# Two graph layers on one core: the order of transposes, reloads and stores at the end, and of gathers before the first regrouped batch

## The chip, the cores and the metric

The kernel runs on one core of a Trainium2 chip. The metric is the device time of one execution in microseconds (us), the median of several runs. A profiled execution is one more run with the hardware profiler on; its span goes from the first to the last instruction. Engines are named as in the profile: PE (TensorE, with PEld for its weight loads), DVE (VectorE), ACT (ScalarE), POOL (GpSimd) and SP (SyncE). A small q behind a name (SPq, ACTq, POOLq) is that engine's queue issuing a DMA.

## What is computed

Per batch (32 of them), x is 512 rows by 512 columns, f32. Two layers, each with a norm and a relu ahead and a residual add behind:

```
h = max(layernorm(x), 0);  x = x + (adj @ h) @ W0 + b0          # layer 0
h = max(layernorm(x), 0)
scores = q @ k.T / 8 + (1 - adj) * -1e9                         # per head
x = x + (softmax(scores) @ v) @ Wo + bo                         # layer 1
```

adj holds values from 0 to 1 off a sparse pattern. In layer 1 the mask weighs every missing piece of adj with 1e9, so each row attends to the one column where its adj is largest (the kernel looks at the data and takes this path only where the gap is wide enough). Layer 1 is then a choice of rows: row i gets `h[idx[i]] @ (Wv @ Wo)` plus a constant row, which the kernel calls `cvo`.

## The kernel before, in words

Rows sit on the 128 partitions, so a batch of x is four tiles of 128x512 ("chunks"). `xs` holds five batches of x in SBUF, `X[b] = xs[b % 5]`.

**Stages of a batch b.** Norm of x, then `aggregate` (adj @ h, into `yT`), then `layer0` (yT @ W0, added onto x), then the second norm into `h1`. `put_h` stores h1 to DRAM (`hs_d`). Only some 336 of the 512 rows are ever chosen by layer 1, so `get_h` reads these alone back into `hc`, `transpose_h` turns them on DVE, and `layer1` computes z for them. `put_z` turns z on DVE and stores it to DRAM (`z_d`) with four DMAs for each of two pieces of columns; `finish` gathers z rows by index onto x, and `store` writes x out.

**Products.** Most products go through `product` (L524 to L558), a fast scheme of seven pieces of eight matmuls: p1, p5, u2, c11, c22, c12, c21, in three PSUM banks u, v, w. c21 accumulates on u, so its matmuls (L528) wait until c22 has been taken out of u by DVE (`take_onto` L584 for layer 0, `take_z` L574 on DVE and L576 on ACT for layer 1).

**The order.** It is written out by hand. For each loop turn b, `put(batch, step, f)` hangs work on one of 21 steps: 0 to 6 lie in `layer0(b)`, 7 to 13 in `aggregate(b + 1)`, 14 to 20 in `layer1(b - 1)`. The work of step i is issued after the matmuls of piece i and ahead of the taking of piece i. Each engine runs its own instructions strictly in that order. Every POOL gather or scatter is also tied by `behind` to the taking of the piece before it.

**Regrouped batches.** Batches 0 to 4 (`FIRST` is 4) use x in its natural order. Later ones gather the rows of x in an order found on the chip (`plan.xi`), in which adj has empty blocks; `spread` (L645, L648, L651) then multiplies only `plan.ap` (four chunks of adj regrouped) and `plan.ag` (three small extra tables), with `HG`, the normed form of three extra gathered chunks `plan.gx`. `tables` and `tables_g` (L1282) gather ap and ag, `load_g` (L495) gathers gx, `mask_g` (L1331) blanks the unused part of ag on DVE. `lead` (norm for batches 5 and 6) and `NormMore` (from 7 on) norm gx on ACT: their sums are L394 and L997, the offset L404/L405, the relu L379/L1010.

**The end.** For the last batches x is put back to natural order: `turn_back` scatters X[b] to DRAM (`xn_d`, L468, on POOL) and `come_back` loads it again (L478, on SP). In turn 31, after `layer0(31)`, the seven pieces of `layer1(29)` and then of `layer1(30)` run. There is no further layer 0, so layer 1 of batch 31 is done row by row: `put_h(31)` stores h (L679), `get_all` gathers the chosen rows of h for all 512 rows (L495, `h<-hs,pi`), `transpose_all(r)` turns a chunk on PE (L711) and copies it out on ACT (L712), and `layer1_rows` multiplies (L723) and adds onto x (L728), after `add_cvo` (L715) has added the constant row. In between it adds the z of batches 29 and 30, which `fetch` gathered into `sel` and `yT` (`add_z`, L784), and every finished chunk is stored by SP (L510).

Of the kernel before, what the change touches and what calls it, by code (L numbers as in the profile page):

```python
# [408 lines left out]
def single_path(ctx: ExitStack, tc: tile.TileContext, x, adj, out, kept, room):  # L409
    nc = tc.nc  # L410
    B, N, D = x.shape
    C, DC = N // P, D // P
# [44 lines left out]
    def run_phase(batches, sparse, small, ps_m, ps_t):  # L457
# [256 lines left out]
        def add_cvo(b, c):  # L714
            nc.vector.tensor_add(X[b][:, c, :], X[b][:, c, :], cvo)  # L715

        def layer1_rows(b):
            for r in range(C):
                bank = ps_m.tile([P, D], F32, name="mm")
                for d in range(DC):  # L720
                    if d == 2 and r + 1 < C:
                        transpose_all(r + 1)
                    nc.tensor.matmul(bank, hs[1][:, d, r * P:(r + 1) * P], wvo[:, d, :], start=(d == 0),  # L723
                                     stop=(d == DC - 1))
                if sparse:
                    add_cvo(b, r)
                x_r = X[b][:, r, :].rearrange("p (q c e) -> p q c e", q=4, c=4)
                nc.vector.tensor_add(x_r, bank.rearrange("p (c q e) -> p q c e", q=4, c=4), x_r)  # L728
                if sparse and r == 0:
                    for c in range(C):  # L730
                        add_z(B - 3, c, nc.sync)
                    fetch(B - 2)
                store_rows(b, r, nc.sync)
                for i in range(2):
                    if not sparse:
                        add_z(B - 3 + r // 2, 2 * (r % 2) + i, nc.sync if r < 2 else nc.scalar)
                    elif 0 < r < C - 1:
                        add_z(B - 2, 2 * r - 2 + i, nc.sync)
# [24 lines left out]
        def put_z(b, s0, s1):  # L763
            zr = hc_t if b == B - 2 else zr_t
            nc.vector.transpose(zr[:, s0:s1, :].rearrange("p s (c e) -> p s c e", c=4),
                                zt(b)[:, :, 32 * s0:32 * s1].rearrange("p c (s j) -> p s c j", j=32))
            rows = z_d[b % 3].rearrange("(s j) (q f) -> q j s f", j=32, q=4)
            for q in range(4):
                eng = nc.scalar if q > 1 and b == B - 2 else nc.sync
                eng.dma_start(rows[q][:, s0:s1, :], zr[32 * q:32 * q + 32, s0:s1, :])  # L770

        def place_of(b, c):
# [31 lines left out]
        for b in batches:  # L804
            todo = [[] for _ in range(21)]

            def put(batch, step, f, *args):
                if 0 <= batch < B:
                    todo[step].append(lambda: f(batch, *args))

            if sparse and b <= FIRST + 1:
                for j in range(3):
                    put(b + 1, 1 + j, lambda b, j: lead.stats(j), j)
                put(b + 1, 3, lambda b: lead.power())
                put(b + 1, 4, lambda b: lead.offset())
                for j in range(3):
                    put(b + 1, 4 + (j + 1) // 2, lambda b, j: lead.relu(j), j)
            if sparse:
                for j, step in enumerate((15, 17, 19) if b == FIRST else (6, 7, 8) if b == FIRST + 1 else (4, 5, 6)):
                    put(b + 2, step, load_g, [j])  # L820
# [10 lines left out]
                put(b + 2, 0, load_x)  # L831
            if b == B - 1:
                for c in range(C):
                    put(b - 2, 17 + c if sparse else 15, fetch, [c])
            elif b < B:
                for c, step in enumerate((9, 11, 13, 15) if sparse and b == FIRST + 1 else (7, 9, 11, 13) if sparse else
                                         (4, 5, 6, 7) if ordered and b == FIRST - 1 else (1, 2, 3, 4)):
                    put(b - 2, step, finish, [c])
            elif not sparse:
                put(b - 2, 1, fetch)  # L840
# [2 lines left out]
            if b > 0 and not sparse and not (ordered and b > FIRST - 3):  # L843
                put(b + 3, 15, load_x)
            if ordered and b == FIRST - 1:
                for j in range(3):
                    put(b + 2, 18 + j, load_g, [j])
            if not sparse:
                for i, step in enumerate((0, 1, 2, 3) if b != 1 else (1, 2, 3, 4)):
                    put(b + 1, step, h0_sum, i)  # L850
# [36 lines left out]
            if b < B - 1:  # L887
                put(b, 20 if not several else 17, get_h)
            elif not sparse:
                put(b, 13, get_all)  # L890
                for c in range(C):
                    put(b, 15 + c, add_cvo, c)
            elif b == B - 1:
                for c in range(C):
                    put(b, 13 + c, get_all, [c])
                    put(b, 7 + c, turn_back, [c])
                    put(b - 1, 2 * c, turn_back, [c])
                put(b - 1, 8, come_back)
                put(b, 15, come_back)
            if sparse and b == B - 2:  # L900
                for c in range(C):
                    put(b - 1, c, turn_back, [c])
# [10 lines left out]
            if b == 0:  # L913
                put(2, 1, lambda b: ahead.append(ln0(b, kind)))
                for c, step in enumerate((1, 1, 2, 2)):
                    put(2, step, lambda b, c: ahead[0].stats(c), c)
            else:
                put(b + 2, 4 if sparse else 8, lambda b: ahead.append(ln0(b, kind)))
                for c, step in enumerate((9, 10, 13, 13)):
                    put(b + 2, step, lambda b, c: ahead[0].stats(c), c)  # L920
                if kind is NormMore:
                    put(b + 2, 4, lambda b: ahead[0].more(plan.gx, plan.HG, 3))
                    for i, step in enumerate((13, 15, 17, 17, 18, 18)):
                        put(b + 2, step, lambda b, i: ahead[0].more_stats(i), i)
                    put(b + 2, 20, lambda b: ahead[0].more_power())
            put(b + 2, (17 if sparse else 15) if b > 0 else 11, lambda b: ahead[0].power())
# [10 lines left out]
                    put(0, 8, lambda b, i: sum_b(nc, w0_t, w0_s, i), i)  # L937
                    put(0, 9, lambda b, i: sum_a(nc, wvo_t, wvo, i), i)
            if b == B - 1:
                put(b, 19, lambda b: transpose_all(0))  # L940
            if b == 1:
                tables = []
                put(1, 0, lambda b: tables.append(places()))
# [73 lines left out]
class Plan:  # L1017
# [315 lines left out]
    def schedule(self):  # L1333
        def at(b, step, f, *args):
            self.steps.setdefault(b, []).append((step, lambda ps_t, behind: f(*args)))

        def pe(b, step, f, *args):
            self.steps.setdefault(b, []).append((step, lambda ps_t, behind: f(ps_t, *args)))

        def move(b, steps, f):  # L1340
            for i, step in enumerate(steps):
                self.steps.setdefault(b, []).append((step, lambda ps_t, behind, i=i: f(behind, i)))

        at(0, 0, self.load)
        at(0, 0, self.constants)
        at(0, 3, self.constants2)
        for c in range(4):
            at(0, 3 + c // 2 * 4, self.nonzero, c)
            at(0, 8 + c // 2, self.nonzero_t, c)
        at(0, 8, self.key_r)  # L1350
        for c in range(4):
            at(0, 11, self.diagonal, self.m, c)
            at(0, 12, self.diagonal, self.mt, c)
        pe(0, 11, self.rank_pe)
        at(0, 12, self.pick_r)
        k = 21
        for r in range(2):
            for go, then in ((self.sources, self.known), (self.reach, self.key_1), (self.rank_pe, self.pick_1),
                             (self.rank_pe, self.pick_2)):
                pe(*divmod(k, 21), go)  # L1360
                at(*divmod(k + 1, 21), then)
                k += 3
        at(*divmod(k - 1, 21), self.classes)
        pe(*divmod(k, 21), self.sources)
        at(*divmod(k + 1, 21), self.outside)
        k += 3
        pe(*divmod(k, 21), self.numbers)
        for i, f in enumerate((self.positions, self.positions_2, self.positions_3, self.slots)):
            at(*divmod(k + 1 + min(i, 2), 21), f)
        pe(*divmod(k + 4, 21), self.row_pe, self.pos)  # L1370
        at(*divmod(k + 5, 21), self.row_save, self.posd)
        for c in range(4):
            at(*divmod(k + 4 + c // 2, 21), self.place_onehot, c)
            at(*divmod(k + 6 + c // 2, 21), self.slot_onehot, c)
        k += 9
        pe(*divmod(k, 21), self.lists)
        at(*divmod(k + 1, 21), self.indices)
        move(2, (17, 18, 19, 20), self.rows)
        for m in range(4):
            pe(3, 4 + m, self.turn, m)  # L1380
        at(3, 6, self.save_at, 0)
        at(3, 8, self.save_at, 2)
        move(3, (11, 13, 15, 17), self.tables)
        move(4, (0, 1, 2), self.tables_g)
        for j in range(3):
            at(4, 4 + j, self.mask_g, j)
        move(5, (14, 16, 18, 20), self.look_1)
        at(6, 4, self.whole_pi)
        pe(6, 5, self.row_pe, self.pqf)
        at(6, 6, self.row_save, self.tab2)  # L1390
        move(6, (14, 16, 18, 20), self.look_2)
        at(7, 5, self.packed, self.pq, self.place)
        at(8, 5, self.packed, self.pi, self.home)
# [261 lines left out]
```

## Time and profile before

| | us |
|---|---|
| median of three runs | 1024.74 (1020.9, 1024.74, 1027.37) |
| the profiled execution's own time | 1019.28 |
| its span | 1017.5 |
| start and end around the span | 1.8 |
| PE busy, and its share of the span | 990.3, 97% |
| DVE busy | 801.1 |
| ACT busy | 585.5 |
| POOL busy | 589.7 |

From turn 6 to turn 30 one loop turn takes 28.82 us. The DMA engines are busy in eight to nine tenths of most slices. PE's granted clock is full except for three stretches (from 235.2 us for 3.4 us, from 986.1 us for 6.8 us, and the last 7 us). The page's rows give, for a group of instructions, the busy time, the mean of one in ns, and the idle time ahead of them with what ended it.

### The profile page before, as it was taken

To read this page: it belongs to the slowest core of one execution; us is meant where nothing else is said; L and a number is where in the kernel's file an instruction comes from. 1 tells how busy PE (TensorE), PEld (TensorE's weight loads), DVE (VectorE), ACT (ScalarE), POOL (GpSimd) and SP (SyncE) were. 2 spreads that over 40 slices of the span, in tenths; PEclk is the share of its full clock that TensorE was granted. 3 is DMA by queue.
4 is the path that set the end of the run, shared out by engine and by line. 5 is a ranking of instruction groups with operands and counts; after the bars stand their busy time and mean duration, and the time that the engine had idled before them with its cause. 6 is when DMAs were issued, how large, how long until landed. Compare 5 with 4: busy or idle time off the path is not lost.

```text
span 1017.5 us, 17277 instructions
## 1 busy us (share of the span) xinstructions
PE 990.3 (97%) x5627; PEld 888.4 (87%) x5627; DVE 801.1 (79%) x1792; ACT 585.5 (58%) x1282; POOL 589.7 (58%) x666
## 2 busy tenths in 40 slices
PE   8999999998999999999999999999999999999986
PEld 7468888898999999999999999999999999999872
DVE  5998888667888777778887777778887777788754
ACT  3766455556765555567655555667655555676230
POOL 1033266656666666666666666666666666666552
PEclk9999999999999999999999999999999999999988
DMA  9314668888887888898888888888888888888886
GB/s 297 114 65 134 119 191 233 211 220 223 223 206 187 215 221 207 226 223 216 213 195 205 214 215 214 227 220 216 202 195 213 215 206 226 227 214 216 204 302 224
DMA packets 163035, 210.99 MB, mean 207 GB/s; under 512 B 16684, under 2 KB 104504, under 8 KB 162936
## 3 DMA queue, kind: packets, MB, share of 16 engines
q0 software_dynamic: 44544, 120.10, 48.5%
q1 hardware_dynamic: 116920, 88.29, 29.9%
q10 hardware_dynamic: 1472, 1.41, 0.4%
q8 instruction: 46, 0.75, 0.3%
q14 instruction: 53, 0.43, 0.2%
HBM read 124.60 MB, written 85.14 MB: 206 GB/s over the span
## 4 chain that ended last, share of the span: by engine, by line
PE 75%; DMA 5%; DVE 2%; ACT 2%; issue 1%; POOL 0%; SPq 0%; POOLq 0%; DVEq 0%
PE mm L528 53%; PE mm L648 13%; PE mm L651 7%; PE mm L645 2%; DMA z<-hc 1%; DMA hc<-hs 1%; DMA at<-in_x_dram,gi 1%; DMA ap<-in_adj_dram,xi 1%; DMA yT<-z,phome 1%; DMA z<-zr 1%; ACT h L379 1%; DMA hs<-h,dest 0%; ACT yT L656 0%; DMA x<-xn 0%; ACT ph L394 0%
## 5 line engine op out<-in xcount | busy, mean ns | idle before, releaser
L584 DVE TENSOR_TENSOR x<-mm,x 128x512 f32<-128x512 f32 x217 | 148.7, 686 | 133.9 <-PE mm L528 131.8
L495 POOL DMA_INDIRECT x<-z,pplace x96 | 153.4, 1598 | 81.8 <-ACT yT L656 40.9
L379 ACT ACTIVATE h<-x,off,rstd 128x512 f32<-128x512 f32 x256 | 196.1, 804 | 7.1 <-DVE off L370 3.9
L528 PE MATMUL mm<-w_t,sel 128*128 128x256 f32 x744 | 171.6, 380 | 1.0 <-DVE x L584 1.0
L365 ACT ACTIVATE rstd<-mv,eps 128x2 f32<-128x2 f32 (+1 forms) x90 | 26.3, 292 | 247.8 <-DVE mv L362 247.7
L361 DVE BATCH_NORM_STATS2 st<-x 128x6 f32<-128x512 f32 x234 | 157.6, 673 | 2.5 <-DMA x<-in_x_dram 1.5
L528 PEld LDWEIGHTS mm<-w_t,sel 128*128 128x128 f32 x744 | 140.7, 190 | 21.0 <-DVE x L584 2.0
L648 PE MATMUL mm<-ap,h 128*128 128x256 f32 x648 | 157.8, 380 | 0.0
L495 POOL DMA_INDIRECT x<-in_x_dram,xi x108 | 103.7, 960 | 73.8 <-DVE x L584 38.4
L512 POOL DMA_INDIRECT out_dram<-x,xi x96 | 120.4, 1254 | 37.3 <-DVE zs L574 20.8
L648 PEld LDWEIGHTS mm<-ap,h 128*128 128x128 f32 x648 | 114.9, 191 | 11.1
L495 POOL DMA_INDIRECT at<-in_x_dram,gi x81 | 76.7, 946 | 74.5 <-DVE st L361 26.3
L528 PE MATMUL mm<-w_s,yT 128*128 128x256 f32 x496 | 117.3, 379 | 0.8 <-ACT zs L576 0.8
L528 PE MATMUL mm<-hTs,wvo_t 128*128 128x168 f32 x720 | 115.0, 309 | 2.9 <-ACT zs L576 2.1
L528 PEld LDWEIGHTS mm<-hTs,wvo_t 128*128 128x128 f32 x720 | 106.5, 192 | 3.9 <-ACT zs L576 3.0
L576 ACT ACTIVATE zs<-mm,cvo_c 128x168 f32<-128x168 f32 x240 | 83.0, 398 | 39.0 <-PE mm L528 38.6
L528 PEld LDWEIGHTS mm<-w_s,yT 128*128 128x128 f32 x496 | 92.8, 190 | 12.3 <-ACT zs L576 1.0
L651 PEld LDWEIGHTS mm<-ag,adjT 128*128 128x128 f32 x648 | 89.3, 191 | 5.6
L651 PE MATMUL mm<-ag,adjT 128*128 128x128 f32 x648 | 89.7, 275 | 0.0
L623 DVE TENSOR_TENSOR x<-x,b_r 128x512 f32<-128x512 f32 x124 | 84.0, 678 | 0.0
L528 PE MATMUL mm<-hT,wvo 128*128 128x168 f32 x480 | 78.6, 307 | 0.0
L656 ACT COPY yT<-mm 128x512 f32<-128x512 f32 x108 | 61.6, 571 | 28.1 <-PE mm L651 27.9
(323 smaller groups left out, 1682.4 us busy)
## 6 DMA issues: line engine op xcount, KB each, us to landing
hc<-hs SPq DMA_DIRECT2D x124, 176.0 KB, 5.7
z<-zr SPq DMA_DIRECT2D x120, 96.0 KB, 3.9
hs<-h SPq DMA_DIRECT2D x52, 192.0 KB
z<-zr SPq DMA_DIRECT2D x120, 80.0 KB, 2.9
hs<-h SPq DMA_DIRECT2D x52, 160.0 KB, 3.0
out_dram<-x SPq DMA_DIRECT2D x32, 256.0 KB, 3.1
x<-in_x_dram SPq DMA_DIRECT2D x12, 256.0 KB, 4.4
x<-xn SPq DMA_DIRECT2D x12, 256.0 KB, 5.0
```

The lines of the kernel that those rows point to most:

```text
L361: self.nc.vector.bn_stats(st, self.src[:, self.chunks[i], :])
L365: self.nc.scalar.activation(self.rstd[:, 0:len(self.chunks)], self.mv[:, :, 1], AF.Sqrt, bias=self.eps)
L379: self.nc.scalar.activation(dst, src, AF.Relu, bias=self.off[:, i:i + 1], scale=self.rstd[:, i:i + 1])
L495: return behind(nc.gpsimd.indirect_dma_start(out=dst, out_offset=None, in_=rows, in_offset=bass.IndirectOffsetOnAxis(ap=at, axis=0), **more))
L512: stored = behind(nc.gpsimd.indirect_dma_start(out=out_rows, out_offset=bass.IndirectOffsetOnAxis(ap=plan.xi[:, b, c:c + 1], axis=0), in_= ...
L528: nc.tensor.matmul(bank[:, m, 0:half], lhs[:, k, m * P:(m + 1) * P], rhs[:, k, :], start=(first and m == 0 and k == 0), stop=(k == 1), ski ...
L576: taken = nc.scalar.activation(dst[:, m, :], bank[:, m, :], AF.Identity, bias=cvo_c[:, 2 * i + m:2 * i + m + 1])
L584: return nc.vector.tensor_add(dst, bank, dst)
L623: nc.vector.tensor_add(X[b][:, c, :], X[b][:, c, :], b0_r)
L648: nc.tensor.matmul(two(bank, j), H0[b][:, j, cols], two(plan.ap[:, j, :], j), start=False, stop=False, skip_group_check=True)
L651: nc.tensor.matmul(bank[:, j * P:(j + 1) * P], extra[:, j - 1, cols], plan.ag[:, j - 1, j * P:(j + 1) * P], start=False, stop=(j == C - 1) ...
L656: tick(nc.scalar.copy(yT[:, d, :], bank))
```

## The change

1. Turn 3 (`b == FIRST - 1`): `load_g(5)` goes from steps 18, 19, 20 to 15, 17, 18; the third and fourth gather of `tables` go from steps 15 and 17 to 19 and 20.
2. Turns 4 and 5: the offset of `lead` goes from step 4 to 5, its relus from 4, 5, 5 to 5, 6, 6 (the relu of j is at the first step plus (j + 1) // 2).
3. Turn 5: the first two of the extra sums of `NormMore` go from steps 13 and 15 to 15 and 16.
4. Turn 31: all four `get_all` at step 13 (13 to 16 before); `come_back(30)` from step 8 to 16; the four `fetch(29)` at step 20 (17 to 20 before); `transpose_all(0)` from step 19 to turn 32; `come_back(31)` from step 15 to turn 32.
5. Turn 32, step 1: `transpose_all(0)`, `come_back(31)` and all four `add_cvo(31)`, which leave `layer1_rows`.
6. `put_z(30)`: all four stores of a piece on SP; two of them were on ACT.

```diff
@@ layer1_rows
-                if sparse:
-                    add_cvo(b, r)
                 x_r = X[b][:, r, :].rearrange("p (q c e) -> p q c e", q=4, c=4)
@@ put_z
-                eng = nc.scalar if q > 1 and b == B - 2 else nc.sync
+                eng = nc.scalar if q > 1 and b == B - 2 and not sparse else nc.sync
@@ run_phase
-                put(b + 1, 4, lambda b: lead.offset())
+                put(b + 1, 5, lambda b: lead.offset())
                 for j in range(3):
-                    put(b + 1, 4 + (j + 1) // 2, lambda b, j: lead.relu(j), j)
+                    put(b + 1, 5 + (j + 1) // 2, lambda b, j: lead.relu(j), j)
...
-                    put(b - 2, 17 + c if sparse else 15, fetch, [c])
+                    put(b - 2, 20 if sparse else 15, fetch, [c])
...
             if ordered and b == FIRST - 1:
-                for j in range(3):
-                    put(b + 2, 18 + j, load_g, [j])
+                for j, step in enumerate((15, 17, 18)):
+                    put(b + 2, step, load_g, [j])
...
-                    put(b, 13 + c, get_all, [c])
+                    put(b, 13, get_all, [c])
                     put(b, 7 + c, turn_back, [c])
                     put(b - 1, 2 * c, turn_back, [c])
-                put(b - 1, 8, come_back)
-                put(b, 15, come_back)
+                put(b - 1, 16, come_back)
...
-                    for i, step in enumerate((13, 15, 17, 17, 18, 18)):
+                    for i, step in enumerate((15, 16, 17, 17, 18, 18) if b == FIRST + 1 else (13, 15, 17, 17, 18, 18)):
...
             if b == B - 1:
-                put(b, 19, lambda b: transpose_all(0))
+                put(b, 20, lambda b: None if sparse else transpose_all(0))
+            if sparse and b == B:
+                put(b - 1, 1, lambda b: transpose_all(0))
+                put(b - 1, 1, come_back)
+                for c in range(C):
+                    put(b - 1, 1, add_cvo, c)
@@ Plan.schedule
-        move(3, (11, 13, 15, 17), self.tables)
+        move(3, (11, 13, 19, 20), self.tables)
```

## The prediction, on record before the result

> **What bounds the kernel now.** I read the page first: PE is busy 97% of the span, so only time in which PE stands still, or work after its last matmul, can be won. The waits of PE say where it stands still; the three largest all lie in stretches that the change touches (waits, count, longest):
>
> ```profile
> PE pt L711 <- DMA h<-hs,pi: 4.8, 1, 4.8
> PE mm L528 <- ACT zs L576: 2.8, 2, 2.1
> PE mm L528 <- DVE x L584: 2.5, 3, 1.5
> ```
>
> The timeline (start, duration, engine, in brackets the idle time ahead and what ended it) shows the 1.5 us in turn 4:
>
> ```profile
> 185.89 0.63 ACT L394 ACTIVATE ph<-at 128x512 bf16<-128x512 f32 x1 [2.69 <-DMA at<-in_x_dram,gi]
> ...
> 189.29 0.18 DVE L404 RECIPROCAL rstd<-rstd 128x3 f32<-128x3 f32 x1 [2.99 <-ACT rstd L401]
> ...
> 189.77 0.68 DVE L584 TENSOR_TENSOR x<-mm,x 128x512 f32<-128x512 f32 x1
> ...
> 190.51 1.99 PE L528 MATMUL mm<-w_t,yT 128*128 128x256 f32 x8 [1.49 <-DVE x L584]
> ```
>
> The gx gathers land late, ACT's sums end late, DVE waits 2.99 us in lead's offset, and the taking of c22 queued behind it holds PE's c21. In turn 5 an extra sum (L997) sits on ACT ahead of p1's taking (L576), for which u2 waits:
>
> ```profile
> 233.71 0.63 ACT L997 ACTIVATE adjT<-at 128x512 f32<-128x512 f32 x1
> ...
> 234.80 0.69 ACT L576 ACTIVATE zs<-mm,cvo_c 128x168 f32<-128x168 f32 x2
> ```
>
> At the end it is no longer PE that counts. PE stands still 4.8 us for the h gather, but what closes the span is a row of transfers and the DVE adds behind them:
>
> ```profile
> 983.71 0.98 POOL L495 DMA_INDIRECT h<-hs,pi  x1 [8.08 <-DMA z<-zr]
> 984.89 0.84 DVE L765 STREAM_TRANSPOSE hc<-h0s 128x640 f32<-128x640 f32 x1 [0.30 <-POOL h0s L760]
> 988.79 1.11 PE L711 MATMUL pt<-ident,h 128*128 128x128 f32 x4 [4.81 <-DMA h<-hs,pi]
> 989.70 2.45 PE L528 MATMUL mm<-adjT_s,wvo 128*128 128x168 f32 x8
> 990.16 0.83 ACTq L770 DMA_DIRECT2D z<-hc  x2
> 992.91 0.98 DVE L765 STREAM_TRANSPOSE hc<-h0s 128x768 f32<-128x768 f32 x1 [7.17 <-ACT h0s L576]
> 998.65 1.18 POOL L495 DMA_INDIRECT yT<-z,phome  x1 [5.15 <-DMA z<-hc]
> 1007.32 0.69 DVE L784 TENSOR_TENSOR x<-yT,x 128x512 f32<-128x512 f32 x1 [2.38 <-DMA yT<-z,phome]
> 1011.32 0.69 DVE L728 TENSOR_TENSOR x<-mm,x 128x512 f32<-128x512 f32 x1
> ```
>
> c21 of layer1(30) sits on PE behind the stalled transposes; z of 30 needs c21; the yT gather needs z; the last adds need yT. Between 264 and 956 us PE has no gap over 0.25 us: time won before stays won there.
>
> **Part 1, the gx gathers sooner, offset a step later (turns 3 and 4).** POOL issues the same seven gathers, spaced as before; gx gets the slots of 172.6, 175.7 and 177.0 us, the last two tables those of 178.2 and 179.5. A gather issued at 176.96 landed at 181.6, so ACT's six sums run from 178.4 to about 184 and the 2.99-us wait goes. Next late is mask_g(0), also ahead of c22's taking: its ag gather ends at 188.42 by the trace's completion events, and its slot is not moved. So 188.5, plus 0.19 to the taking's start, 0.68, 0.06: c21 starts near 189.4 instead of 190.51, **-1.1**. Offset and relus then stand ahead of c12's taking, which no early matmul needs; mask_g(2), for which L651 waits, comes at about 192.7, and PE gets to L651 at 192.8. Cost of the late tables: they land like the gathers now in their slots, by 187.3; L645 needs ap from 191.2, so 3.9 us of cover. Were it gone, PE would wait the difference. DVE has 0.3 us of offset put into its chain, so the stores of h(4) come only 0.8 sooner, and by 223 us (`hc<-hs` landing) that chain leads: **-0.8** carried on. Bounds: 0 (ag later) to -1.4.
>
> **Part 2, turn 5.** Without L997 ahead of it, p1's taking starts 0.6 sooner (ACT still has the yT copy at 234.33): u2 at 235.54 - 0.8 - 0.6. **-0.6**; the sum then delays p5's taking, needed only by c12. The shifted offset of turn 5 saves under 0.3 where DVE waits 1.62 for L401; taken as 0. Here a rule bears on it. The clock row:
>
> ```profile
> 235.20:238.60 3.40, 3.06 (x11) 3.06 (x12) 3.34 (x6) 1.98 (x7) 2.93 (x4) 0.50 1.00 184
> ```
>
> (PE, PEld, DVE, ACT, POOL busy, granted clock, DMA share, GB/s): half clock, so u2 and c11 took 3.87 us for 2.28 at full clock, 1.6 lost. The Trainium skill ("TensorE: Matmul & The Clock Gate", Part 1) has the half rate come after an idle window of some 3.4 us; by that a gap of 2.06, or of 1.5, shouldn't trip it, and nothing is to be won. The trace differs: 2.06 and 0.70 within one such time were enough. With 1.5 and 0.7 left it may go either way; I take a fifth, **-0.3**, bounds 0 to -1.6. Early stages together -1.7.
>
> **Part 3, the end.** (a) `come_back(30)` out of the way of h: four loads of 262 KB, 1.05 MB, ran ahead of `hs<-h` in SP's queue at 396 GB/s (976 to 981 us): 2.6 us. Scatters of xn share the engines, so I take 2.3: gather of h at 981.4 (bounds 1.0, 2.6). (b) c21 follows c12 at once: 983.9 for 989.70, taken by ACT by 986.0. (c) The blanking of h0s (L760) was behind one h gather on POOL and now is behind four, 1.27 each: 986.4, and z's first transpose waits for it, 1.5 later than now. Both transposes (0.84 and 0.98) end at 988.3 instead of 993.9. (d) Eight z stores on SP. The skill ("DMA: Bandwidth & Descriptors", Queues, rings and completion order) says each DMA engine takes turns between the queues it has work for, which speaks against this part: ACT's two stores had a queue of their own, now they stand behind come_back(30)'s 1.05 MB, issued from 981.5. By the rule that costs up to 2.7 us against a free queue; by the rows ACT's pair came out only at 990.16, behind the copy after the stalled transposes, and the second at 993.92. I take issues from 987.4 to 991, landing at 994.3 (now 997.9; the last issue at 995.10 took 2.8, I allow 3.3). (e) fetch(29) starts on POOL at 986.6 (now 988.79), so POOL is free; fetch(30) at 995, **3.7 sooner**. (f) `come_back(31)` goes from 983.44 behind the z stores to 991.5: x(31) lands near 997. DVE now has four add_cvo (0.68 each) queued ahead of all adds of `layer1_rows`, and they wait for it: row 0 at 997.3 (now 996.51). From there DVE does row 0, four adds of z(29) (2.5), row 1, two adds of z(30), row 2, two, row 3: 4 x 0.69 + 2.5 + 2.5 = 7.8, if yT is there: 1005.1; yT's last piece at about 1005.3 (now by 1009.3, less 3.7) makes it 1006.6. PE starts rows at 988 and needs 16 (991.7 to 1007.7 now): 1004, covered. Last store issued at 1006.7 for 1012.04, **-5.3**. (g) Twelve stores of 262 KB need 0.67 each at 390 GB/s, 8.1; from 999.3 with 0.5 MB of yT still to come (1.3), and some idle: 1009.3 for 1014.5. I take **-4.7** for the end: bounds -1 (x(31) at 1001) and -7 (transfers without a gap: 11.6 MB from 974 on at 390 GB/s are 29.7 us, plus some 3.5 for z's short pieces, 1007.5).
>
> **Sum.** -1.7 - 4.7 = -6.4 on the span, 1017.5 to 1011.1; the profiled execution has 1.8 around it, 1019.28 to 1012.9. The median of the runs shown is 5.5 above the profiled one, so 1024.74 - 6.4 = **1018.3**.
>
> **Rivals.**
> *Transfers bound the tail.* The same bytes are moved, nothing fewer. For: the DMA share is 1.04 from 976 to 981 and 1.00 from 986 to 991. Against: 0.63 from 996 to 1001, 0.65 after 1006, room to fill. If queues collide so that yT is only 1.5 sooner, the end gives 2 and the early part 1.7: 1021.
> *More than counted.* The clock stays full in turn 5 (1.3 more) and the tail closes at its bound (2.3 more): 1014.7 or lower. Against: DVE's chain alone needs until 1005.
> *Slower: x(31) too late.* Every add of the last layer now waits behind add_cvo, and x(31) behind eight z stores and a reload. On the present axis the end is then x(31)'s landing plus 0.7 + 7.8 + 2.5 and about 3 to the span's end: it is 1017.5 when x(31) lands at 1003.5, and with the early 1.7 it decides against the change from 1005.2, 8.2 later than I count. If z's eight stores slip behind the reload and the fetches until 1005 and x(31) with them to 1008, the span grows by 2.8 and the time is near 1027.5. Against: in the present run loads issued at 983.44 landed within six us among the same gathers.
> *It doesn't do what it says in the early part.* ag instead of gx holds DVE and `hc<-hs` leads anyway: early 0, end 4.7, 1020; inside the main range.
>
> **How the numbers follow.** Main case (early and end as summed, with its own range 1015.5 to 1021) 56%; transfer-bound tail 19%; more than counted 17%; x(31) late 8%. The spread between runs, 0.6% (1020.9 to 1027.37) lies on top. The range 1012.5 to 1025.5 leaves out the worst of the late case and the best of "more than counted". About 1% is what a measurement of this kernel tells from no change: faster needs under 1014.5, most of the "more" case and a little of the main, 18%; slower needs over 1035, only far in the late case, 5%; the rest 77%.
>
> **What would show it.** Right: c21 of layer0(4) near 189.4; u2 of turn 5 near 234.1; c21 of layer1(30) at about 983 with no transposes ahead; the first yT gather near 993 to 995 on the new axis; first out store near 996 to 999 and the last near 1005. Wrong: a wait of DVE's L715 on `x<-xn` past 1000, a PE wait on ap at L645, or an hs gather not sooner than 983.

## The result, and the profile after

| | before | after |
|---|---|---|
| median of 22 runs each, one chip | 1023.1 | 1022.93 |
| range | 1018.38 to 1027.37 | 1018.11 to 1028.14 |
| ratio, 95% interval | | 1.0003 (0.9986 to 1.0019) |
| profiled execution, its span | 1019.28, 1017.5 | 1018.11, 1016.4 |

No change: not the 6.4 us less that were forecast. Two later measurements of the same two kernels (below) gave 0.997 and 0.9978, some 2 to 3 us less. The bulk of the forecast is missing in all three.

The waits of PE after. The 4.8 us for the h gather are gone, and 1.5 us of waiting for the copy of the transposes are left; but the two rows on the takings are as long as before:

```profile
PE mm L528 <- ACT zs L576: 3.1, 3, 1.7
PE mm L528 <- DVE x L584: 2.8, 3, 1.7
...
PE mm L723 <- ACT h L712: 1.5, 1, 1.5
```

The end, from three answers of the timeline of after (POOL, PE, DVE), with what answers to the rows shown of before:

```profile
980.63 1.02 POOL L495 DMA_INDIRECT h<-hs,pi  x1 [5.71 <-DVE zr L763]
...
997.66 0.95 POOL L495 DMA_INDIRECT yT<-z,phome  x1 [5.16 <-DMA x<-xn]
```

```profile
984.45 1.30 PE L528 MATMUL mm<-adjT_s,wvo 128*128 128x168 f32 x8
985.59 0.60 PE L711 MATMUL pt<-ident,h 128*128 128x128 f32 x4
987.72 1.98 PE L723 MATMUL mm<-wvo,h 128*128 128x512 f32 x4 [1.54 <-ACT h L712]
```

```profile
987.09 1.70 DVE L763 STREAM_TRANSPOSE hc<-h0s 128x640 f32<-128x640 f32 x2
998.25 2.64 DVE L715 TENSOR_TENSOR x<-x,cvo 128x512 f32<-128x512 f32 x4 [9.46 <-DMA x<-xn]
1000.82 0.68 DVE L726 TENSOR_TENSOR x<-mm,x 128x512 f32<-128x512 f32 x1
...
1007.48 0.68 DVE L726 TENSOR_TENSOR x<-mm,x 128x512 f32<-128x512 f32 x1
```

The h gather starts 3.1 us sooner, c21 5.2 sooner (984.45 for 989.70), but the first yT gather only 1.0 sooner. (Its bracket names `x<-xn`, but what it waits for is z: in every profile it starts 0.8 to 1.0 us after the last store of z(30) has landed, whenever x(31) lands.) DVE, which did rows and adds from 996.5 on, stands 9.5 us for x(31) and starts its last chain at 998.25; row 0 comes 4.3 us *later*. The last store is issued at 1009.93 for 1012.04.

The early turns of this execution hold something that no other profile here has: takings that start late though PE is done. DVE at 216.91 takes c11, whose matmuls (214.03, 1.89 long) had ended a microsecond before; it had idled 3.64 us, and PE then waits 1.74 for the PSUM bank:

```profile
214.03 1.89 PE L528 MATMUL mm<-w_s,yT 128*128 128x256 f32 x8
216.91 1.29 DVE L584 TENSOR_TENSOR x<-mm,x 128x512 f32<-128x512 f32 x2 [3.64 <-PE mm L528]
217.66 1.99 PE L528 MATMUL mm<-w_t,sel 128*128 128x256 f32 x8 [1.74 <-DVE x L584]
```

Such takings stand at 150, 173 to 177, 217, 255, 594 and 973 to 986 us. Turns 3 and 6 (from the first matmul of `layer0` to that of the next) were 37.9 and 30.9 us long for 36.1 and 28.9 in a later profile of the same kernel. The trace of this one is also incomplete: it lacks a seventh of PE's completion events (1099; the others have 1291 to 1295), a quarter of ACT's and two fifths of those of the DMAs (9866, where the others have 16338 to 16429), so what its brackets name is less sure than elsewhere. And this execution, at 1018.11 us, is the fastest of its 22, so the late takings are not what makes that median high. They recur in none of the fourteen profiles that follow, so I don't put them down to the change. Whether they are the chip's, the profiler's or chance stays open.

### The profile page after: what moved, and what is told of

It reads as the page before. It is cut to its first block, busy times and chain, and to the rows that moved or that the text cites. A ratio compares the mean times of both kernels' runs of the same rounds, so it can differ in the third digit from the quotient of the medians.

```text
span 1016.4 us, 17276 instructions
## 1 busy us (share of the span) xinstructions
PE 987.2 (97%) x5627; PEld 886.0 (87%) x5627; DVE 800.8 (79%) x1792; ACT 585.5 (58%) x1282; POOL 590.3 (58%) x666
## 3 DMA queue, kind: packets, MB, share of 16 engines
q10 hardware_dynamic: 704, 1.05, 0.3%
## 4 chain that ended last, share of the span: by engine, by line
PE 86%; DVE 5%; DMA 3%; ACT 2%; issue 1%; SPq 1%; DVEq 0%; ACTq 0%
PE mm L528 60%; PE mm L648 13%; PE mm L651 7%; PE mm L645 2%; PE mm L271 1%; PE mm L669 1%; PE mm L150 1%; DMA x<-in_L_gnn_Wv_dram 1%; DMA ap<-in_adj_dram,xi 1%; ACT h L379 1%; DVE st L361 1%; DMA x<-xn 1%; DMA x<-z,place 1%; DMA hc<-hs 0%; DVE x L623 0%
## 5 line engine op out<-in xcount | busy, mean ns | idle before, releaser
L495 POOL DMA_INDIRECT at<-in_x_dram,gi x81 | 77.5, 957 | 69.2 <-DVE st L361 22.8
L576 ACT ACTIVATE zs<-mm,cvo_c 128x168 f32<-128x168 f32 x240 | 83.1, 399 | 41.0 <-PE mm L528 30.4
L656 ACT COPY yT<-mm 128x512 f32<-128x512 f32 x108 | 61.6, 571 | 30.4 <-PE mm L651 30.2
```

What stands on the lines that cost most here:

```text
L495: return behind(nc.gpsimd.indirect_dma_start(out=dst, out_offset=None, in_=rows, in_offset=bass.IndirectOffsetOnAxis(ap=at, axis=0), **more))
L576: taken = nc.scalar.activation(dst[:, m, :], bank[:, m, :], AF.Identity, bias=cvo_c[:, 2 * i + m:2 * i + m + 1])
L656: tick(nc.scalar.copy(yT[:, d, :], bank))
```

## The experiments

Ratios are to the kernel before, run beside it (its medians there: 1018.6 to 1019.6 us). Times "at the end" count from the issue of the second store of h (`hs<-h`, L679; 976.24 before, 975.52 after), so that the early turns drop out; landings are read from the trace's completion events (16 to a DMA).

### The two halves: e1_early, e2_end

e1_early is the kernel before with parts 1 to 3; e2_end has parts 4 to 6 only.

> The kernel before with parts 1 to 3 alone (turns 3 to 5); the end as before. Theory A (the early sum holds, and the end gives it no loss): 1.7 us less than before, ratio 0.998, with c21 of layer0(4) starting some 1.1 us sooner relative to turn 3, and layer0(5) to layer0(7) some 1.7 sooner than before. Theory B (the early stages give back what they win: the profile after shows layer0(4) 1.8 and layer0(5) 2.5 us quicker, but turn 3 slower by 2.0 and turn 6 by 2.0, where takings start 0.5 to 2.5 us after PE is done): if these late takings come from the change they stand at the same places here (173 to 180 us, 217 us, 255 us) and the time is that of before within 0.5 us; if they are chance of one execution, they are gone or stand elsewhere, and the first turns show theory A's numbers.

> The kernel before with parts 4 to 6 alone (the end); the early turns as before. Theory A (x(31) comes late and DVE is parked at add_cvo, so the end wins 0.3 us instead of 4.7): within 0.7 us of before; the last store is issued at most 2.5 us sooner, DVE stands some 9 us ahead of add_cvo. Theory C (the end wins its 4 to 5 us and the early part loses them): 4 to 5 us less than before, ratio 0.9955, and DVE's wait ahead of add_cvo is short.

Measured: e1_early 0.9982 (0.997 to 0.9993), that is -1.8 us; e2_end 0.9992 (0.9974 to 1.001), -0.8. Theory A in both. The early steps by their rows in e1_early: the mask, not the offset, stands last ahead of c22's taking, and c21 follows with no gap:

```profile
188.33 0.29 DVE L1331 TENSOR_SCALAR ag<-ag,valid 128x128 f32<-128x128 f32 x1 [1.63 <-DMA ag<-atd,gi]
188.53 0.68 DVE L584 TENSOR_TENSOR x<-mm,x 128x512 f32<-128x512 f32 x1
189.13 0.17 DVE L404 RECIPROCAL rstd<-rstd 128x3 f32<-128x3 f32 x1
189.27 1.99 PE L528 MATMUL mm<-w_t,yT 128*128 128x256 f32 x8
```

In turn 5 the taking of p1 is ahead of the sum; the wait for hT's sums is 1.20 here for 0.70 before:

```profile
231.34 1.38 PE L528 MATMUL mm<-hTs,wvo_t 128*128 128x168 f32 x8 [1.20 <-DVE hTs L341]
...
233.43 0.69 ACT L576 ACTIVATE zs<-mm,cvo_c 128x168 f32<-128x168 f32 x2
234.01 0.64 ACT L997 ACTIVATE adjT<-at 128x512 f32<-128x512 f32 x1
234.18 1.41 PE L528 MATMUL mm<-hTs,wvo_t 128*128 128x168 f32 x8 [1.45 <-ACT zs L576]
```

Over the profiles (first matmul of `layer0` to the next), turn 4 takes 30.68 and 31.02 us in the two without the early parts and 29.45 in the mean of thirteen with them (28.9 to 30.9: the late gathers vary); turn 5 takes 33.76 and 33.68, and 32.77 (31.7 to 35.4). The wait for hT's sums is no constant either: 0.36 to 1.96 us in the thirteen, 0.58 and 0.70 in the two.

### Where the end is held: e3_rows, e4_back

e3_rows puts add_cvo back, e4_back loads x(31) ahead of z(30)'s stores:

```diff
# e3_rows
+                if sparse:
+                    add_cvo(b, r)
                 x_r = X[b][:, r, :].rearrange(...)
...
-                for c in range(C):
-                    put(b - 1, 1, add_cvo, c)
# e4_back
                 put(b - 1, 16, come_back)
+                put(b, 17, come_back)
...
-                put(b - 1, 1, come_back)
```

> The changed kernel with add_cvo put back into the loop of rows (one ahead of each row's add), come_back(31) still behind the eight stores of z(30). Theory A1 (what costs is that DVE does four add_cvo in a row before anything else): first store some 2 us sooner, the time 1 to 2 us less than the changed kernel. Theory A2 (what costs is that x(31) itself is loaded late; each add_cvo waits for the load either way): DVE still stands some 9 us ahead of the first add_cvo, the first store comes 1.5 to 2 us sooner (three add_cvo fewer ahead of it) but the end moves by less than 1 us, since the stores after it are bound by transfers. Theory C (transfers bound the tail): no change.

> The changed kernel with come_back(31) right behind come_back(30), ahead of the stores of z(30). Theory A2 (late x(31) is what ate the end's gain): x(31) lands near 989 us, DVE no longer waits ahead of add_cvo, row 0 is added by about 993 for 1000.8, out stores start some 7 us sooner and fill the gap in the transfers, and the span ends 3 to 5 us sooner than that of the changed kernel: ratio to before 0.995 to 0.997. Theory C (transfers bound the tail, the same bytes in another order): within 1 us of the changed kernel. Against A2: z(30)'s stores would then wait for 1.05 MB more ahead of them (up to 2.7 us), and fetch(30) with them, which would leave a gain of 1 us or none.

Measured: 0.9967 (0.9954 to 0.9979) and 0.9973 (0.9957 to 0.999). In e3_rows DVE still waits 8.1 us for x(31); the first store comes 2.3 us sooner at the end than in a0_after (22.3 for 24.6), the last one when it did (34.1 for 33.9): A2's numbers. But e4_back, which cures the late x(31) (row 0 at 20.3 for 23.3 in a0_after, the unaltered change), doesn't win A2's 3 to 5 us: its end is 39.8 against 40.3. There z(30) pays. The waits of SP's queue in e4_back:

```profile
SPq L768 <- DMA x<-xn: 6.1, 7, 1.3
```

Seven of z(30)'s eight stores wait, each for the landing of a load: the program hands SP's and ACT's DMAs eight semaphores in turn (100 to 107 in the trace), so a ninth is issued only when the eighth before it has landed. The last store goes out at 19.7 for 14.6, and the first yT gather at 23.0. So late x(31) and late z(30) are two chains of about the same length, and curing one of them brings little.

### The whole change again: a0_after, a1_after

> The changed kernel once more, on the chip of these runs, with a new profile. Parts 1 to 3 alone gave 0.9982 and parts 4 to 6 alone 0.9992. If the parts add up (theory A), the whole is at 0.997 to 0.998 of before here, and its profile has no takings that start 0.5 to 2.5 us after PE is done. If the first comparison (1.0003, interval 0.9986 to 1.0019) holds as it stands, the parts get in each other's way: 1.000, and the late takings at 173 to 180, 217, 255 and 973 to 986 us are there again (theory B).

> The changed kernel a third time. Its first comparison gave 1.0003 (0.9986 to 1.0019), its second 0.997 (0.9957 to 0.9982), and the sum of its two halves 0.9974. If the second holds: 0.996 to 0.998, and a profile without takings that start late. If the first holds: 0.999 to 1.001, and the late takings are there again.

Measured: 0.997 (0.9957 to 0.9982) and 0.9978 (0.9964 to 0.9992); the halves added give 0.9974. No taking starts late in either profile. The 1.0003 of the first measurement lies outside both intervals, though its own (from 0.9986 on) overlaps that of a1_after; there the kernel before, too, took 4 us more, and I have no run that says why.

### What delays z(30): e5_z_act, e6_back30_late, e7_no_back30, e9_no_fetch29, e11_fetch29_last

All five start from e3_rows. e7_no_back30 leaves out the reload of x(30) and e9_no_fetch29 the gathers of fetch(29); both do less than the kernel must, and only measure a time.

```diff
# e5_z_act
-                eng = nc.scalar if q > 1 and b == B - 2 and not sparse else nc.sync
+                eng = nc.scalar if q > 1 and b == B - 2 else nc.sync
# e6_back30_late (e7_no_back30: the first line alone)
-                put(b - 1, 16, come_back)
+                put(b - 2, 1, come_back)      # turn 32, behind come_back(31)
# e9_no_fetch29 (and e11_fetch29_last)
-                    put(b - 2, 20 if sparse else 15, fetch, [c])
# e11_fetch29_last, layer1_rows: behind fetch(B - 2), and after the last row
-                    for c in range(C):
-                        add_z(B - 3, c, nc.sync)
+                    fetch(B - 3)
...
+                    elif r == C - 1:
+                        add_z(B - 3, 2 * i, nc.sync)
+                        add_z(B - 3, 2 * i + 1, nc.sync)
```

> The kernel with add_cvo in the loop of rows, and the third and fourth store of each piece of z(30) on ACT's queue again (part 6 undone). Theory Q (in SP's queue the eight stores stand behind the reload of x(30) and wait for free places, and so land late): on ACT's queue four of them are out sooner, z(30) lands 1 to 2.5 us sooner, the first yT gather starts that much sooner, and the span ends 0.5 to 2 us sooner than with all on SP. Theory C (the DMA engines are busy all the time from the h gathers to the last store, so that an order of transfers moves little): the first yT gather moves by less than 1 us and the span by less than 0.5 us.

> The kernel with add_cvo in the loop of rows, and come_back(30), 1.05 MB, put behind the stores of z(30) and behind come_back(31). Theory Q: the stores of z(30) have nothing ahead of them in SP's queue, land some 2.5 us sooner, and fetch(30) with them; the span ends 1 to 2.5 us sooner. Theory C: the 1.05 MB are only moved to where they stand in the way of the yT gathers and of the first out stores; the first yT gather comes sooner, the last one lands when it did, and the span moves by less than 0.7 us either way.

> The kernel with add_cvo in the loop of rows, and come_back(30) left out: x(30) keeps its regrouped order, so that the output of batch 30 isn't the reference's; 1.05 MB less are moved in the tail. Theory C (transfers bound the tail): the span ends by about the time of these loads sooner, 2.0 to 2.7 us. Theory A2 (the chain of x(31), adds and stores bounds it): less than 0.7 us. The same as with come_back(30) put late, if its place is what matters (theory Q).

> The kernel with add_cvo in the loop of rows, and the four gathers of fetch(29) left out: sel isn't filled, so that the output of batch 29 isn't the reference's, and 1.05 MB less are moved, from POOL's queue, at the time at which z(30) is stored. It measures the disputed term: how long z(30)'s stores take to land. With come_back(30) left out they still took 6.5 us from the last issue to the first yT gather. If the gathers of fetch(29) are what stretches them: 3.3 to 4 us, as in the kernel before, and the first yT gather 2 us sooner. If the short pieces of the stores themselves set it, or x(31): 5.5 to 6 us as now.

> The kernel with add_cvo in the loop of rows, fetch(29) put behind fetch(30) on POOL, and the four adds and stores of x(29) behind the last row's. Place theory (the gathers of fetch(29) lie just where z(30)'s stores are in flight, and stretch them): the first yT gather comes 3.3 to 4 us after the last issue of z(30), not 5.4 to 6, the last add of z(30) 2 to 3 us sooner; what it brings depends on sel, which then lands last, near 31 us after the second store of h, and four stores follow it: the span within 1 us of the one with fetch(29) early. Bytes theory (leaving fetch(29) out won time because 1.05 MB less were moved): the yT gather comes as late as before, since x(31) and the stores take the room, and the span is the same or longer by what the late adds cost, 1 to 2 us.

| | ratio, 95% interval | last z(30) store issued, landed | first yT gather | last yT landed | end |
|---|---|---|---|---|---|
| e3_rows | 0.9967 (0.9954 to 0.9979) | 14.7, 19.0 | 20.1 | 32.0 | 39.5 |
| e5_z_act | 0.9985 (0.9972 to 0.9997) | 17.5, 20.0 | 20.9 | 29.2 | 41.7 |
| e6_back30_late | 0.9973 (0.9961 to 0.9985) | 14.5, 20.9 | 21.7 | 33.3 | 40.8 |
| e7_no_back30 | 0.9963 (0.9949 to 0.9977) | 14.3, 20.0 | 20.8 | 33.1 | 40.7 |
| e9_no_fetch29 | 0.9915 (0.9893 to 0.9937) | 14.7, 17.2 | 18.3 | 28.6 | 36.0 |
| e11_fetch29_last | 0.9976 (0.9965 to 0.9987) | 15.7, 18.0 | 19.1 | 30.4 | 41.0 |

The reload of x(30) that stands ahead of z(30) in SP's queue costs z nothing: without it (e7) or with it behind (e6) z lands later, if anything. So theory Q falls, and so does the plain form of C: 1.05 MB less moved is not 2 to 2.7 us less. The gathers of fetch(29), from POOL's queue, are what stretches z's stores: from last issue to landing 4.3 to 6.4 us with them (e5 apart, whose last store goes out only at 17.5, when the second of sel's four pieces is landing), 2.6 and 2.3 without them or with them last. The issue of the stores on SP and the first yT gather on POOL, in e3_rows:

```profile
983.57 3.87 SPq L770 DMA_DIRECT2D z<-hc  x8
992.36 0.95 POOL L495 DMA_INDIRECT yT<-z,phome  x1 [4.83 <-DMA x<-xn]
```

The same in e9_no_fetch29 (the second store of h is 0.5 us earlier there):

```profile
983.02 3.89 SPq L770 DMA_DIRECT2D z<-hc  x8
990.07 0.95 POOL L495 DMA_INDIRECT yT<-z,phome  x1 [7.95 <-DMA x<-xn]
```

That agrees with the rule of the Trainium skill named in the prediction ("DMA: Bandwidth & Descriptors", Queues, rings and completion order: each DMA engine takes turns between queues). I had weighed it for ACT's queue; it bites from POOL's. It isn't proved by this: in e3_rows x(30) had landed (13.5) before z's last store was issued (14.7), while sel was in flight until 19.6, and plain sharing of the engines would look alike. Leaving fetch(29) out takes 3.5 us from the end; putting it last only moves the cost: sel lands at 33.2, its four stores close the span, and the end is 1.5 us later than in e3_rows.

Part 6 proves good, against the rule's advice. Undone, it gives 1018.06 us, beside 1016.42 of the changed kernel: with two stores of each piece on ACT, a store waits there for one of the eight semaphores, and the copy of the first transposes is queued behind it. ACT and PE in e5_z_act:

```profile
988.85 3.35 ACTq L770 DMA_DIRECT2D z<-hc  x2
992.24 0.58 ACT L712 COPY h<-pt 128x512 f32<-128x512 f32 x1 [4.43 <-DMA z<-hc]
```

```profile
992.88 3.78 PE L723 MATMUL mm<-wvo,h 128*128 128x512 f32 x4 [7.46 <-ACT h L712]
```

### Using the time in which DVE waits: e8_z29_first, e8_again, e10_back31_act

sel (fetch(29)) has landed by 19.4 to 20.6, ahead of x(31)'s last piece and long ahead of yT, yet its adds stand behind x(31) on DVE. e8_z29_first is e3_rows with them ahead; e10_back31_act also loads x(31) from ACT's queue.

```diff
# e8_z29_first, e8_again
         def layer1_rows(b):
+            for c in range(C if sparse else 0):
+                add_z(B - 3, c, nc.sync)
...
                 if sparse and r == 0:
-                    for c in range(C):
-                        add_z(B - 3, c, nc.sync)
                     fetch(B - 2)
# e10_back31_act
-                put(b - 1, 1, come_back)
+                put(b - 1, 0, come_back, nc.scalar)
```

> The kernel with add_cvo in the loop of rows, and the four adds and stores of x(29) ahead of the first add_cvo, so that they don't wait for x(31). Theory D (what closes the tail is a chain: z(30)'s stores land 5.9 us after the last issue, yT 7.5 us after its last gather, the last adds and stores, all of them stretched by the other transfers in flight): four of the twelve out stores are issued some 5 us sooner, in the time in which DVE now waits, and stand less in yT's way; last store 1 to 2.5 us sooner. Theory C (transfers busy throughout): less than 0.7 us. Against both: the stores come at the time at which z(30)'s stores and x(31) are in flight and push yT back, 0 to 1 us slower.

> The kernel with the adds and stores of x(29) first, once more, since its first comparison had few runs (0.9943, 0.9922 to 0.9964): if the gain over the changed kernel is real, again 0.993 to 0.996 of before and 1 to 3 us less than the changed kernel run beside it; if the first look was a lucky one, 0.9965 to 0.9975 like the kernel with add_cvo in the loop of rows.

> The kernel with the adds and stores of x(29) first, and come_back(31) on ACT's queue ahead of the copies of the transposes, not behind the eight stores of z(30) in SP's. If each queue has its own share of the DMA engines (theory Q), x(31) lands 3 to 4 us sooner and z(30) at most 1 us later, rows are added 3 us sooner, last store 0.5 to 2 us sooner than with x(29) first alone. Theory D: z(30) lands later by what x(31) takes from it (1 to 2.5 us), yT with it, and the time is the same or up to 1.5 us longer.

Measured: e8 0.9943 (0.9922 to 0.9964, six runs) and again 0.996 (0.9944 to 0.9976), 1014.61 us beside 1016.94 of the changed kernel (by the means of these runs 2.0 us less, 0.8 to 3.1): the best of both kernels and all variants that leave nothing out. Against e3_rows (0.9967, from another chip) it is not clear of noise. e10_back31_act 0.9976 (0.9964 to 0.9989): x(31) on ACT takes semaphores that z(30) then waits for, z's first store goes out at 15.1 for 10.8, and the gain is gone.

What e8 fills is seen in the DMA share (last column but one) over three stretches of 5 us from 10 us after the second store of h on. The unaltered change (a0_after):

```profile
985.53:990.53 5.00, 4.26 (x14) 1.94 (x13) 1.70 (x2) 1.17 (x2) 3.65 (x5) 1.00 1.01 362
990.53:995.53 5.00, 5.00 (x16) 2.44 (x15) 0.00 (x0) 0.59 (x1) 0.20 (x1) 1.00 1.04 358
995.53:1000.53 5.00, 5.00 (x16) 2.33 (x15) 4.28 (x7) 0.59 (x1) 3.62 (x4) 1.00 0.65 211
```

The same three stretches in e8_again, and DVE there:

```profile
984.86:989.86 5.00, 4.33 (x16) 2.37 (x17) 1.71 (x2) 1.17 (x2) 3.92 (x6) 1.00 1.03 375
989.86:994.86 5.00, 5.00 (x16) 2.35 (x15) 2.38 (x4) 0.59 (x1) 0.12 (x1) 1.00 1.07 359
994.86:999.86 5.00, 5.00 (x16) 2.48 (x15) 3.06 (x5) 0.59 (x1) 3.20 (x3) 1.00 1.06 395
```

```profile
990.44 0.69 DVE L784 TENSOR_TENSOR x<-sel,x 128x512 f32<-128x512 f32 x1 [3.59 <-DMA sel<-z,phome]
...
994.56 0.69 DVE L784 TENSOR_TENSOR x<-sel,x 128x512 f32<-128x512 f32 x1 [1.05 <-DMA sel<-z,phome]
995.41 0.69 DVE L715 TENSOR_TENSOR x<-x,cvo 128x512 f32<-128x512 f32 x1 [0.17 <-DMA x<-xn]
...
1001.02 0.69 DVE L784 TENSOR_TENSOR x<-yT,x 128x512 f32<-128x512 f32 x1 [2.73 <-DMA yT<-z,phome]
...
1006.88 0.69 DVE L730 TENSOR_TENSOR x<-mm,x 128x512 f32<-128x512 f32 x1
```

In the change the engines are full for 10 us and then stand a third idle, because DVE has nothing to hand to the stores until x(31) is there; in e8 the stores of x(29) fill that hole.

## Why the prediction was wrong, step by step

**Early part, forecast -1.7: right.** e1_early measured -1.8 (-3.1 to -0.7). Turn 4: in e1_early c21 starts 10.5 us into the turn for 12.1 before, 1.6 sooner for a forecast of 1.1, with ag's mask last, as said (that its 189.27 lies so near the forecast 189.4 is in part luck, as turn 4 began 0.4 later there); -1.4 in the mean of the profiles for -1.1. Of the thirteen profiles with the early parts eight have no gap ahead of c21, the others 0.3 to 1.6 us. Turn 5: -0.95 in the mean for -0.6 - 0.3. The stall for p1's taking fell from 2.06 to 1.45, the 0.6 of the forecast, and is at most 1.45 in all thirteen; ahead of it the wait for hT's sums varies, the way `hc<-hs` leads that the prediction named.

**End, forecast -4.7: wrong.** e2_end measured -0.8 (-2.6 to 1.0); by the profiles the end is at 40.3, 39.2 and 40.2 for 41.3, and 41.9 with the old end in e1_early. The forecast's steps, in us after the second store of h:

| | before | forecast | a0_after, a1_after, e2_end |
|---|---|---|---|
| (a) first h gather | 7.5 | 5.2 | 5.2, 5.2, 5.2 |
| (d) last z(30) store issued | 18.9 | 14.8 | 14.6, 14.5, 15.5 |
| (d) z(30) landed | 21.6 | 18.1 | 19.4, 19.6, 20.8 |
| (e) first yT gather | 22.4 | 18.8 | 20.5, 20.6, 21.8 |
| (f) x(31) landed | 15.1 | 20.8 | 22.6, 22.1, 23.3 |
| (f) row 0 added | 20.3 | 21.1 | 23.3, 22.8, 23.9 |
| (f) last piece of yT landed | 32.7 | 29.1 | 31.9, 30.2, 32.1 |
| last store issued | 35.8 | 30.5 | 33.9, 32.8, 33.9 |
| end | 41.3 | 36.6 | 40.3, 39.2, 40.2 |

In this table everything up to the issue of z(30) is right within 0.7 us; every landing is late. The failed step is (d), "landing at 994.3 (... the last issue at 995.10 took 2.8, I allow 3.3)": it took 4.8 to 5.3. The 2.8 came from a place where fetch(29) had all but landed (three of four pieces by 19.0, the last at 20.2, the store at 18.9); the change issues z(30) 4 us sooner, right into these gathers. e9 and e11 show that: 2.6 and 2.3 without them. The same crowd makes x(31) 1.3 to 2.5 late, and row 0, which (f) took right behind "near 997", is 1.7 to 2.8 late. Nearly all of that is the load: the four add_cvo (2.64 us in a row) start when its first piece lands and end 0.6 us after its last, where (f) had 0.3. Their place isn't what decides: with add_cvo row by row the last store goes out when it did.

Of the 2.6 to 3.7 us by which the end misses, 1.3 to 2.7 are there when z(30) lands. Another 0.4 to 1.7 come between the first yT gather and the last store, where the forecast had 11.7 us; no run takes that part to pieces, and its cause stays open.

**The rivals.** "Transfers bound the tail" gave nearly the measured size (yT 1.5 sooner, the end 2 us) by its words "if queues collide". As a bound by bytes it falls (e7_no_back30, and a share of 0.65 from 995.5 to 1000.5). x(31) did come late, but at 998.4 to 999.5 on the axis of before and not at 1005, so it cost part of the gain and no more; with it early (e4_back) z(30) took its place as the late one. "More than counted" was out of reach: its tail needed transfers without a gap.

**The half clock.** The forecast took a fifth of the 1.6 us, since it could not tell what the gate looks at. The profiles narrow it down (below). The 1.6 is too large: at full clock u2 and c11 took 2.48 us there in all nine profiles that kept it, not 2.28, so 1.4 were lost.

## What to carry to other kernels

When a transfer is issued sooner, read its landing time from a row with the same traffic around it; the time of its old place belongs to its old neighbours. Before moving a load past a store, count how many DMAs of that program are in flight: here the ninth waits for the first, whatever it carries. Where an engine is parked for data, look for work further down its queue whose data has landed: with the four adds and stores of x(29) handed out first, and add_cvo back in the rows, the kernel ran 2.3 us under the changed one beside it (medians).

## What the runs showed of the hardware

**The clock gate counts a fixed window, and one that is about half idle can be enough.** In each trace all clock changes lie on a grid of 3.41 us. Around the two stalls of turn 5 I read PE's busy time (first number behind the length) in the window that ends at the change, or could have, and the clock (third from the end) in it and in the next. Before, a1_after, and e6_back30_late, which stayed at full clock:

```profile
231.77:235.18 3.41, 1.38 (x8) 1.15 (x8) 3.31 (x9) 3.41 (x9) 2.69 (x2) 1.00 0.91 199
235.18:238.60 3.42, 3.06 (x11) 3.06 (x12) 3.36 (x6) 2.00 (x8) 2.95 (x4) 0.50 1.00 185
```

```profile
227.49:230.90 3.41, 1.45 (x10) 1.22 (x9) 3.24 (x11) 3.00 (x6) 2.54 (x3) 1.00 0.67 197
230.90:234.31 3.41, 2.55 (x10) 2.12 (x9) 3.34 (x9) 3.41 (x10) 2.94 (x4) 0.50 0.97 190
```

```profile
228.55:231.96 3.41, 1.75 (x10) 1.52 (x11) 3.31 (x9) 3.41 (x9) 2.81 (x3) 1.00 0.95 199
231.96:235.37 3.41, 3.41 (x25) 3.22 (x24) 3.41 (x7) 3.38 (x12) 2.95 (x4) 1.00 1.01 192
```

In these windows of turn 5, PE busy 1.35, 1.38, 1.38, 1.45, 1.54 and 1.61 us (40 to 47%) was followed by the half clock, 1.75 and 1.77 (51 to 52%) was not. Busy time alone is not the whole rule: in turn 4 of e2_end a window on the grid with one gap of 1.83 us and 1.59 busy (47%) was followed by full clock:

```profile
189.36:192.78 3.42, 1.59 (x8) 1.07 (x7) 2.17 (x7) 2.92 (x7) 0.77 (x1) 1.00 0.91 328
192.78:196.19 3.41, 3.41 (x22) 3.15 (x21) 3.31 (x9) 0.90 (x3) 1.41 (x3) 1.00 0.54 153
```

So near 47% it goes either way, and these traces don't show what decides. The Trainium skill ("TensorE: Matmul & The Clock Gate", Part 1) has the free-running window, but an idle one before the rate falls; here a half-idle one did it. Depending on how the two stalls of turn 5 (0.36 to 1.96 and at most 1.45 us) fall across the grid, it trips in 4 of the 13 profiles with the early parts, and in both of those without. In a1_after and e7_no_back30 the half clock then held for two windows, and turn 5 took 35.0 and 35.4 us, for 31.7 to 33.1 in the other eleven; their waits for hT's sums, 1.96 and 1.88, are in that too. How much of the 1% by which runs of one kernel differ comes from such trips is not shown.
